# Last layer: one unread bf16 product ahead of each half score tile and of each bank of distance products

## The chip, the cores and the metric

The program runs on one core of one Trainium2 chip. The metric is the device time of one execution in microseconds; lower is better. A core has five engines with a queue each: TensorE (PE; its weight loads are shown as PEld), VectorE (DVE), ScalarE (ACT), GpSimd (POOL) and SyncE (SP), which here only issues DMAs. An engine works through its queue in order; engines wait for each other through semaphores. TensorE writes into PSUM, which has banks of 512 float32 per partition; VectorE and ScalarE read it.

## The reference: what is computed

Four layers run one after the other over an activation `x` of 4 sequences, 1024 tokens and 128 channels. Each layer is `x = x + s * silu(f)`, where `s` is an attention or a recurrence and `f` a feed-forward block over the normalised `x`. Only the last layer (layer 3) is changed. Its attention has 16 heads of 8 channels, is causal, and adds a term for the relative distance of two tokens:

```python
srel = srel_skew(jnp.einsum('bhnd,hmd->bhnm', qx, ex))      # products with distances, then a shift by rows
qk = (jnp.einsum('bhnd,bhmd->bhnm', qx, kx) + srel) * inv_dim
mask = 1000000000.0 * jnp.triu(jnp.ones((n, n), dtype=x.dtype), 1)
atten = jax.nn.softmax(qk - mask, axis=-1)
out = jnp.einsum('bhnm,bhmd->bhnd', atten, vx).transpose(0, 2, 1, 3).reshape(b, n, d)
return out @ Wp.T + bp
```

The table of distances has 256 entries, so each query tile of 128 tokens needs distance products of 256 columns, while its scores have up to 1024 columns.

## The kernel before

Layers 0 to 2 fill the first part of the span; the first instruction of layer 3's attention on TensorE starts 2151.5 us after the span's start. Layer 3 (`layer3`, L1736) works on 16 groups: 4 sequences (`b`) by 4 sets of heads (`i`), 4 heads at a time (`j`), whose 32 channels each (8 channels split into high and low parts, both in float32r) lie in a 32-row strip of the tiles `q` and `k`. Within a group, 8 query tiles `t` of 128 tokens are taken in the order 7, 0, 6, 1, 5, 2, 4, 3 (L1733); these are the 128 units (L1759).

**Scores.** `scores3` (L2077) goes through a unit's key columns in tiles of 512: two for `t` above 3, one otherwise, so 12 in a group and 192 in the layer. Each tile takes two PSUM buffers `sc` of two banks (L2095), one for heads 0 and 1, one for heads 2 and 3: a half score tile is one such buffer. All `sc` buffers there are is two (L2240), so the products of the next tile (L2097, one for each head, 32 rows by up to 512 columns) can only start when VectorE has read the same half of the tile before. VectorE reads each head's scores, adds the distance term `rel`, and finds the row's minimum of the negated scores (L2106, L2113). ScalarE then takes the exponential (L2120).

**Weights times values.** `transpose` (L1793) has VectorE turn the exponentials into tiles `wT` (L1807), and `weigh3` (L2126) multiplies them by the values with small float32 products into 32-column strips of `po` (L2134). The `wT` tiles have one buffer of each size, so a transpose may wait for earlier products. A float32 product is two instructions on TensorE.

**Distances.** `relative3` (L2021) is called 8 times for each group, seven parts ahead of the unit that needs it (L1862): two PSUM banks `pr` from the three `tr` buffers (L2029), in each two products of 32 rows by 256 columns (L2033), copied to `r` by ScalarE (L2035), stored to HBM (`flat`, L2038 and L2039) and read back in a sheared form as `rel` (`shear3`, L2042, L2054 to L2060), where GpSimd fills the masked parts (L2064).

**Beside these** run the feed-forward block (`ffn3`, L1972) in four pieces in the units of the second group of each sequence, the projections of the next sequence (`begin3`, L1933), and `finish3` and `end3` (L2142, L2158), which close a group and a sequence.

**What sets the order.** The loop of L1839 writes the products of a score tile, then a transpose and part of the weighing, then the comparison of that tile. The framework that builds the program keeps data dependencies and buffer reuse but may place independent instructions of one engine in another order, by its own estimate of when each can run. The trace shows that it does so: the first score product runs at 2155.08 us between distance products, although the source writes seven parts of distances ahead of it (L1785).

Of the kernel before, what the change touches and what calls it, by code (L numbers as in the profile page):

```python
# [11 lines left out]
BF16 = mybir.dt.bfloat16  # L12
# [8 lines left out]
P = 128  # L21
# [1714 lines left out]
def layer3(k, W, x3, out, eps5, ps, first):  # L1736
# [11 lines left out]
    nc, tc = k.nc, k.tc  # L1748
    with ExitStack() as st:
        pool = lambda name, bufs, **kw: st.enter_context(tc.tile_pool(name=name, bufs=bufs, **kw))  # L1750
        p1, p2, temp, dram = pool("l3", 1), pool("l3d", 2), pool("l3r", 3), pool("rel3", 6, space=DRAM)
        pairs = []
        for n in range(2):
            q, kk = p1.tile([P, 1 + T], F32R, tag=f"q{n}", name="q"), p1.tile([P, T], F32R, tag=f"k{n}", name="k")
            nc.vector.memset(q[:, 0:1].bitcast(F32), 0.0)
            pairs.append((q, kk))
        vb = p1.tile([P, 32, 4, 4, 8], F32, tag="vb", name="vb")
        nc.gpsimd.memset(vb, 0.0)
        units = [(b, i, t) for b in range(NB) for i in range(4) for t in ORDER3]  # L1759
        batch, group, flats, rels = {}, {}, {}, {}  # L1760

        def part(h):

            at, h = divmod(h, 8)
            if at < 4 * NB:
                pair = ORDER3[h // 4 * 4 + h // 2 % 2] // 2
                if h % 2 == 0:
                    flats[at, pair] = dram.tile([P, 4, 2, 384], F32, tag="flat", name="flat")
                relative3(k, W, temp, ps, flats[at, pair], group[at]["q"], at % 4, pair, h % 2)

        def ahead(n):
            if n < len(units):
# [2 lines left out]

        def stream():
            for n, (b, i, t) in enumerate(units):
                yield from scores3(k, p1, p2, ps, group[n // 8], rels.pop(n), t)

        batch[0] = {"qk": first["qk"], "vd": first["vd"], "xnT": p1.tile([P, T], F32, tag="xnT", name="xnT")}  # L1780
        nc.sync.dma_start(out=batch[0]["xnT"], in_=first["xnT"])
# [3 lines left out]
        for n in range(7):  # L1785
            part(n)
            if n in (1, 3):
                ahead(n // 2)
# [45 lines left out]

        tiles = [(n, first) for n, (b, i, t) in enumerate(units) for first in range(0, (t + 1) * P, 512)]
        fill = stream()
        next(fill)
        next(fill)
        for x, (n, first) in enumerate(tiles + [(len(units), 0)] * 4):  # L1839
# [8 lines left out]
            b, i, t = units[n]  # L1848
            at, pos = n // 8, n % 8
# [9 lines left out]
            if pos == 0:  # L1859

                next(project, None)
            part(n + 7)  # L1862
            if pos == 2:
                next(project, None)
# [153 lines left out]
        nc.gpsimd.tensor_copy(vb[rows, :, :, a, :], v[rows].rearrange("p n (j d) -> p n j d", d=8))  # L2018


def relative3(k, W, temp, ps, flat, q, i, pair, jp):  # L2021

    nc = k.nc
    r = temp.tile([P, 2, 2, 256], F32, tag="temp", name="r")
    js = (2 * jp, 2 * jp + 1)
    pr = [ps.tile([P, 2, 256], F32, tag="tr", name="pr") for _ in js]  # L2029
    for m in range(2):  # L2030
        for j, to in zip(js, pr):
            at, t = slice(32 * j, 32 * j + 32), 2 * pair + m
            nc.tensor.matmul(to[:, m, :], q[at, t * P : (t + 1) * P], W["emb"][at, i, :], start=True, stop=True)  # L2033
    for n, to in enumerate(pr):
        nc.scalar.copy(r[:, n], to)  # L2035
    rows = flat[:, 2 * jp : 2 * jp + 2].rearrange("p j m u -> p (j m) u")
    r = r.rearrange("p j m u -> p (j m) u")
    nc.sync.dma_start(out=rows[:, :, 0:256], in_=r)  # L2038
    nc.sync.dma_start(out=rows[:, :, 256:384], in_=r[:, :, 0:P])  # L2039
# [34 lines left out]
    return rel  # L2074


def scores3(k, p1, p2, ps, group, rel, t):  # L2077

    nc = k.nc
    q, kk = group["q"], group["k"]
    n = (t + 1) * P
    at = lambda j: slice(32 * j, 32 * j + 32)
    size = "b" if t > 3 else "s"
    S = [(p2 if t > 3 else p1).tile([P, T if t > 3 else 512], F32, tag=f"S{size}{j}", name="neg") for j in range(4)]
    group["S", t] = S
    low = [p2.tile([P, 3], F32, tag=f"low{j}", name="low") for j in range(4)]  # L2090
    least = [3e38] * 4
    plain = max(0, t - 4) * P
    for first in range(0, n, 512):
        last = min(first + 512, n)
        halves = [ps.tile([P, 2, 512], F32, tag="sc", name="score") for _ in range(2)]  # L2095
        for j in range(4):
            nc.tensor.matmul(  # L2097
                halves[j // 2][:, j % 2, 0 : last - first], q[at(j), 1 + t * P : 1 + n], kk[at(j), first:last], start=True, stop=True
            )
        yield "products"  # L2100
        for j in range(4):
            sc = halves[j // 2][:, j % 2]

            neg, m = S[j], low[j]
            if first < plain:
                nc.vector.tensor_scalar(  # L2106
                    neg[:, 0:plain], sc[:, 0:plain], -INV3, None, op0=ALU.mult, op1=ALU.min, accum_out=m[:, 0:1]
                )
                least[j] = m[:, 0:1]
            begin = max(first, plain)  # L2110
            slot = min(t, 4) - t + begin // P
            here = m[:, 1:2] if first == 0 else m[:, 2:3]
            nc.vector.tensor_tensor_reduce(  # L2113
                out=neg[:, begin:last], in0=sc[:, begin - first : last - first],
                in1=rel[:, j, slot : slot + (last - begin) // P, :].rearrange("p s c -> p (s c)"),
                scale=-INV3, scalar=least[j], op0=ALU.add, op1=ALU.min, accum_out=here,
            )
            least[j] = here
            if last == n:
                nc.scalar.activation(  # L2120
                    neg[:, 0:n], neg[:, 0:n], AF.Exp, bias=here, scale=-1.0, accum_out=group["sums"][:, j, t : t + 1]
                )
        yield "compared"
# [70 lines left out]
def tile_kernel(ctx: ExitStack, tc: tile.TileContext, I, out):  # L2194
# [44 lines left out]
    with last, ExitStack() as st:  # L2239
        ps = PsumTags(st, tc, {"sc": 2, "tr": 3, "o": 1}, "ps3")  # L2240
        layer3(k, W3, x3, out, eps5, ps, first)
# [20 lines left out]
```

## Time and profile before

| What | Value |
|---|---|
| Runs shown (3) | 3174.36, 3178.16 and 3178.8 us; median 3178.16 us |
| The profiled execution's own time | 3175.99 us |
| Its span, first to last instruction | 3174.2 us, so 1.8 us lie around it |
| Granted TensorE clock over the span | 0.738 of full |
| Layer 3's stretch from 2150 to 3130 us | 980 us; busy: PE 717.84, PEld 479.63, DVE 770.02, ACT 669.23, POOL 307.24 |
| Granted clock in that stretch | 0.68 |
| DMA in that stretch | busy share 0.77, 235 GB/s |
| Score products in that stretch (L2097) | 756 instructions, 217.5 us busy, mean 588 ns |
| Distance products (L2033) | 512 instructions, 125.8 us busy, mean 426 ns |
| Weighing products (L2134) | 9683 instructions, 254.0 us busy, mean 253 ns |

How to read the profile: an engine's busy time is the time in which at least one of its instructions is recorded as running. The records of products overlap, since each contains a fixed latency and products follow each other into the array. The granted clock is the share of full speed that the chip's throttle allowed TensorE. The view of lines gives for each group of instructions its count, its busy time and mean duration, and then the idle time of the engine just before, with what ended it. The view of waits turns this around: who waited for whom, how long in all, how many times, and the longest.

### The profile page before, as it was taken

The numbers are of one execution on the slowest core, as the hardware profiler recorded it, in microseconds if no ns is written. First come the engines' busy times: TensorE is split into PE (matmuls) and PEld (weight loads), VectorE is DVE, ScalarE is ACT, GpSimd is POOL, SyncE is SP. The second block draws the span as 40 slices with busy tenths as digits, with TensorE's granted clock in tenths as the row PEclk, the third lists the DMA queues.
The fourth block names the chain that finished last, engine by engine and source line by source line (L and its number), as shares of the span: only waits on it lengthen the run. The fifth ranks groups of instructions, "written<-read, shape, count | busy, mean of one in ns | idle before, by whom it ended". The sixth has DMA issues, their size and how long they took to land. (4 is left out here: it accounts for less than half of the span.)

```text
span 3174.2 us, 47753 instructions
## 1 busy us (share of the span) xinstructions
PE 2163.6 (68%) x17039; PEld 1256.8 (40%) x17041; DVE 2291.8 (72%) x5558; ACT 1542.6 (49%) x3300; POOL 1167.5 (37%) x1094
## 2 busy tenths in 40 slices
PE   5777777577887776794543574375777777777865
PEld 2555555232332232562210122253544544544543
DVE  5554544878888786656778888676788797687777
ACT  3554544333333333535432463145765775775773
POOL 3433444144444434123477433232333332323322
PEclk9888888588888887895655566565766666766666
DMA  3000000100000000230334356339588588678772
GB/s 78 16 1 1 1 1 1 35 0 0 0 0 0 7 7 7 103 110 20 74 92 114 123 120 136 100 118 295 174 256 272 176 268 261 197 242 269 215 242 66
DMA packets 334065, 333.13 MB, mean 105 GB/s; under 512 B 25968, under 2 KB 307436, under 8 KB 328196
## 3 DMA queue, kind: packets, MB, share of 16 engines
q1 hardware_dynamic: 332676, 325.90, 34.6%
q10 hardware_dynamic: 1152, 4.19, 0.4%
q8 instruction: 134, 2.20, 0.3%
q14 instruction: 103, 0.84, 0.1%
HBM read 175.31 MB, written 154.14 MB: 104 GB/s over the span
## 5 line engine op out<-in xcount | busy, mean ns | idle before, releaser
L2120 ACT ACTIVATE neg<-neg,low 128x640 f32<-128x640 f32 (+7 forms) x512 | 390.7, 766 | 105.8 <-DVE low L2113 104.6
L1807 DVE STREAM_TRANSPOSE wT<-neg 128x640 f32<-128x640 f32 (+7 forms) x512 | 366.3, 754 | 50.3 <-PE po L2134 45.5
L2064 POOL TENSOR_SCALAR_AFFINE_SELECT rel<-rel 128x512 f32<-128x512 f32 x288 | 180.5, 638 | 551.4 <-DMA rel<-flat 412.6
L2134 PE MATMUL po<-wT,vb 128*32 128x64 f32 (+1 forms) x10240 | 266.2, 253 | 71.9 <-issue 40.8
L2097 PE MATMUL score<-k,q 32*128 32x512 f32 (+3 forms) x768 | 220.5, 587 | 124.6 <-DVE low L2113 121.3
L2134 PEld LDWEIGHTS po<-wT,vb 128*32 128x32 f32 x10240 | 210.9, 134 | 144.5 <-issue 84.1
L2113 DVE CUSTOM_DVE_ANT_0 neg<-score,rel,low 128x128 f32<-128x128 f32 (+3 forms) x448 | 213.0, 510 | 71.4 <-PE score L2097 29.3
L2035 ACT COPY r<-pr 128x512 f32<-128x512 f32 x256 | 135.2, 584 | 126.4 <-PE pr L2033 79.8
L2113 DVE CUSTOM_DVE_ANT_0 neg<-score,rel 128x512 f32<-128x512 f32 (+3 forms) x320 | 150.6, 520 | 50.4 <-POOL rel L2064 21.2
L2097 PEld LDWEIGHTS score<-k,q 32*128 32x128 f32 x768 | 96.8, 247 | 214.1 <-DVE low L2113 139.6
L837 PE MATMUL pg<-xnT,w 128*128 128x512 f32 x256 | 149.1, 666 | 7.1 <-DVE h L841 4.0
L2033 PE MATMUL pr<-emb,q 32*128 32x256 f32 x512 | 125.8, 426 | 39.7 <-ACT r L2035 25.5
L840 ACT ACTIVATE h<-pg 128x512 f32<-128x512 f32 x128 | 75.9, 596 | 157.5 <-PE pg L837 154.1
L790 POOL TENSOR_TENSOR prod<-rest,kv 128x2048 f32<-128x2048 f32 x32 | 145.5, 4598 | 18.4 <-ACT rest L780 18.4
L839 PE MATMUL pu<-xin,w 128*128 128x512 f32 x256 | 140.5, 632 | 12.9 <-DVE h L841 7.4
L828 PE MATMUL po<-h,w 128*128 128x512 f32 x256 | 129.8, 628 | 26.5 <-DVE h L841 26.5
L216 PE MATMUL pt<-ident,three 128*24 128x128 bf16 x64 | 9.2, 295 | 196.6 <-DVE three L213 196.6
L2033 PEld LDWEIGHTS pr<-emb,q 32*128 32x128 f32 x512 | 89.0, 262 | 74.4 <-ACT r L2035 38.9
L433 PE MATMUL px<-hT,xbcT 128*128 128x512 f32 x256 | 115.0, 593 | 0.0
L1086 PE MATMUL ph<-xin,upT 128*128 128x512 bf16 (+1 forms) x126 | 68.3, 572 | 66.4 <-DVE xin L1080 64.0
L1491 PE MATMUL read<-kt,const_sb 128*128 128x128 f32 x256 | 51.1, 372 | 90.3 <-POOL kt L1486 90.3
L785 DVE TENSOR_REDUCE s<-prod 128x128 f32<-128x2048 f32 x32 | 73.1, 2284 | 49.6 <-POOL prod L790 49.6
(633 smaller groups left out, 5775.7 us busy)
## 6 DMA issues: line engine op xcount, KB each, us to landing
flat<-r SPq DMA_DIRECT2D x128, 512.0 KB
rel<-flat SPq DMA_DIRECT2D x112, 512.0 KB
flat<-r SPq DMA_DIRECT2D x128, 256.0 KB
rel<-flat SPq DMA_DIRECT2D x96, 256.0 KB
kt<-kd SPq DMA_DIRECT2D x16, 512.0 KB
qt<-qd SPq DMA_DIRECT2D x16, 512.0 KB
kdc<-kdd SPq DMA_DIRECT2D x16, 512.0 KB
ktc<-ktd SPq DMA_DIRECT2D x16, 512.0 KB
```

Source lines behind the costliest of these rows:

```text
L790: nc.gpsimd.tensor_tensor(prod, attn.rearrange("p (t h g) -> p t h g", t=4, g=16)[:, t].unsqueeze(2).to_broadcast(each), kv[:, t, 1, :].re ...
L828: nc.tensor.matmul(po, W["w2"][:, e, c, :], h[:, c, :], start=(e == 0 and c == 0), stop=(e == 7 and c == 1))
L837: nc.tensor.matmul(pg, W["w1"][:, e, c * P : (c + 1) * P], xnT, start=True, stop=True)
L839: nc.tensor.matmul(pu, W["w3"][:, e, c * P : (c + 1) * P], xin, start=True, stop=True)
L1807: nc.vector.transpose(weights[at, pair][j][:, t % 2, 0 : (t + 1) * P], S[j][:, 0 : (t + 1) * P])
L2033: nc.tensor.matmul(to[:, m, :], q[at, t * P : (t + 1) * P], W["emb"][at, i, :], start=True, stop=True)
L2035: nc.scalar.copy(r[:, n], to)
L2064: nc.gpsimd.affine_select(out=rel[:, :, slot(back), :], in_=rel[:, :, slot(0), :], compare_op=op, fill=fill, base=0, pattern=[[0, 4], [-si ...
L2097: nc.tensor.matmul(halves[j // 2][:, j % 2, 0 : last - first], q[at(j), 1 + t * P : 1 + n], kk[at(j), first:last], start=True, stop=True)
L2113: nc.vector.tensor_tensor_reduce(out=neg[:, begin:last], in0=sc[:, begin - first : last - first], in1=rel[:, j, slot : slot + (last - begi ...
L2120: nc.scalar.activation(neg[:, 0:n], neg[:, 0:n], AF.Exp, bias=here, scale=-1.0, accum_out=group["sums"][:, j, t : t + 1])
L2134: nc.tensor.matmul(o[32 * j : 32 * j + 32, 2 * pair + m.start : 2 * pair + 2, :], vb[:, kb % 4 * NT + kb // 4, j].rearrange("p a d -> p (a ...
```

## The change

A tile `ones` of 512 bf16 columns is filled once by GpSimd at the layer's start, just behind the fill of `vb` (L1758). A function `beat` multiplies the bf16 identity `ident16`, which is there already (L103), by `ones` into a whole PSUM bank. Nobody reads what it writes: the product that follows starts its own sum in the same bank. One beat is written ahead of each half score tile (for heads 0 and 2, into the half's first bank), two at the start of each call of `relative3`, one for each of its two banks. That is 2 x 192 = 384 and 2 x 128 = 256, together 640 beats, each with a weight load of its own.

```diff
         vb = p1.tile([P, 32, 4, 4, 8], F32, tag="vb", name="vb")
         nc.gpsimd.memset(vb, 0.0)
+        ones = p1.tile([P, 512], BF16, tag="ones16", name="ones")
+        nc.gpsimd.memset(ones, 1.0)
+
+        def beat(bank):
+
+            nc.tensor.matmul(bank, k.ident16, ones, start=True, stop=True)
+
...
     pr = [ps.tile([P, 2, 256], F32, tag="tr", name="pr") for _ in js]
+    for to in pr:
+        beat(to.rearrange("p m u -> p (m u)"))
     for m in range(2):
...
         halves = [ps.tile([P, 2, 512], F32, tag="sc", name="score") for _ in range(2)]
         for j in range(4):
+            if j % 2 == 0:
+                beat(halves[j // 2][:, 0])
             nc.tensor.matmul(
```

The other lines of the diff only hand `beat` on to `relative3` and `scores3`.

More of the change, by code (lines that the diff above doesn't have):

```diff
@@ L1768, in part @@
                     flats[at, pair] = dram.tile([P, 4, 2, 384], F32, tag="flat", name="flat")
-                relative3(k, W, temp, ps, flats[at, pair], group[at]["q"], at % 4, pair, h % 2)
+                relative3(k, W, beat, temp, ps, flats[at, pair], group[at]["q"], at % 4, pair, h % 2)
         def ahead(n):
@@ L1777, in stream @@
             for n, (b, i, t) in enumerate(units):
-                yield from scores3(k, p1, p2, ps, group[n // 8], rels.pop(n), t)
+                yield from scores3(k, beat, p1, p2, ps, group[n // 8], rels.pop(n), t)
         batch[0] = {"qk": first["qk"], "vd": first["vd"], "xnT": p1.tile([P, T], F32, tag="xnT", name="xnT")}
@@ L2018, in values3, with relative3 @@
         nc.gpsimd.tensor_copy(vb[rows, :, :, a, :], v[rows].rearrange("p n (j d) -> p n j d", d=8))
-def relative3(k, W, temp, ps, flat, q, i, pair, jp):
+def relative3(k, W, beat, temp, ps, flat, q, i, pair, jp):
     nc = k.nc
@@ L2074, in shear3, with scores3 @@
     return rel
-def scores3(k, p1, p2, ps, group, rel, t):
+def scores3(k, beat, p1, p2, ps, group, rel, t):
     nc = k.nc
```

## The prediction, made before the changed kernel ran

> **What bounds the kernel now.** First the page's busy shares and its slices, then the stretch of layer 3 (2150 to 3130 us) by lines, by waits of VectorE, and by windows.
>
> ```profile
> PE 2163.6 (68%) x17039; PEld 1256.8 (40%) x17041; DVE 2291.8 (72%) x5558; ACT 1542.6 (49%) x3300; POOL 1167.5 (37%) x1094
> ...
> DVE  5554544878888786656778888676788797687777
> ...
> PEclk9888888588888887895655566565766666766666
> ```
>
> The change touches only layer 3, the last 13 of the 40 slices. There VectorE is 70 to 90% busy and TensorE's granted clock is 0.6 to 0.7. In the 980 us VectorE works 770.02 us, more than any other engine. So the end is set by VectorE's work plus its idle time, and the change can act only through that idle time. Its causes:
>
> ```profile
> DVE wT L1807 <- PE po L2134: 45.5, 15, 8.7
> DVE neg L2113 <- POOL rel L2064: 43.5, 13, 12.0
> DVE neg L2113 <- PE score L2097: 31.2, 23, 4.1
> DVE neg L2113 <- issue: 26.9, 12, 3.1
> DVE neg L2106 <- PE score L2097: 20.1, 16, 9.3
> DVE on L2155 <- PE pr L2153: 12.6, 11, 2.7
> ```
>
> Columns: total us, times, longest. TensorE ends 45.5 us of the waits by its weighing products, 51.3 us by score products, 12.6 us by finishing a group. In the 43.5 us, the distance terms come late from HBM; there TensorE is not the cause.
>
> **What the clock follows.** The granted clock is 0.50 or 1.00 and changes only every 3.41 us. Windows cut at those places (columns: PE, PEld, DVE, ACT, POOL busy with counts, clock, DMA share, GB/s):
>
> ```profile
> 2305.40:2308.81 3.41, 3.41 (x86) 2.47 (x76) 1.52 (x7) 0.37 (x1) 1.57 (x2) 0.50 0.65 236
> 2308.81:2312.23 3.42, 3.06 (x18) 1.87 (x16) 3.42 (x10) 3.06 (x6) 3.20 (x4) 1.00 0.38 134
> 2312.23:2315.64 3.41, 1.27 (x5) 0.57 (x4) 3.41 (x14) 2.46 (x5) 1.86 (x3) 0.50 1.11 364
> ...
> 2325.88:2329.29 3.41, 3.41 (x96) 2.74 (x88) 3.41 (x17) 3.39 (x7) 0.56 (x1) 0.50 0.37 108
> 2329.29:2332.71 3.42, 3.42 (x152) 2.56 (x155) 2.89 (x13) 3.38 (x7) 0.00 (x0) 1.00 1.11 228
> ```
>
> The first window is full and the clock rises after it. The second has PE busy 3.06 of 3.42 us, yet the clock falls after it. What differs is how much of the array was used. The second holds 12 distance and 4 score products, each of 32 rows only. Count work in beats: 512 columns once through the whole array are 1; a float32 instruction counts its columns twice (L1983's pairs of 256 columns follow each other every 0.43 us at full clock); 32 rows or 32 columns count a quarter. A score product of 512 columns is then 0.25, a distance product 0.125, a weighing product of 64 columns 0.0625. The first window holds about 6.0, the second 2.3, that of 2325.88 about 5.8. Over all windows of layer 3, a line at 5.0 to 5.2 beats in a window separates "full next" from "half next" with 4 exceptions in 299. That is the working rule here: about 5.1 beats of array work in 3.41 us.
>
> [...]
>
> **Work before and after.** By shapes and counts of the stretch: weighing 545, feed-forward 192 and 96, scores 142, L2166 96, distances 64, the rest 114, together 1249 beats in 287 windows, or 4.35 a window, below the line. The change adds 640 beats, to 6.6 on average. The work is uneven, so I went through the windows, adding one beat at every second score product and two at every fourth distance product. The share of windows above the line goes from 39% to 66%. So the clock should go from 0.68 to about 0.83, not to 1.
>
> **The price of a beat.** The nearest row is layer 2's bf16 product of 512 columns:
>
> ```profile
> L1086 PE MATMUL ph<-xin,upT x126: 376/609/634, 1471.0 to 1917.3; 128*48 128x512 bf16 x64, 128*128 128x512 bf16 x62
> ```
>
> Minimum, median and maximum in ns. The minimum is at full clock, the median at half, so halving adds 609 - 376 = 233 ns: one pass takes about 0.23 us at full clock and 0.47 at half, the rest is latency that overlaps. 640 beats are 149 us at full clock, 301 at half. The weight loads (95 to 151 ns in the same view) lie beside running products, except where the queue stood empty, which the bounds below include. A beat also parts the four score products: four score products of 512 columns now run beside each other (0.50 us for four at 2515.64, full clock); with a beat between the halves only two can.
>
> **Part by part.**
>
> 1. *Beats ahead of scores (384).* TensorE waits there for VectorE to free the half, then does beat and products while VectorE goes on with the other half and with transposes (355.3 us over 192 tiles, 1.85 us a tile). That hides most of them. Going through the 192 tiles, the time between the end of a half's products and VectorE's first use is under 0.25 us in 39 tiles for the first half and in 28 for the second, under 0.45 in 45 and 41. Lengthening each by its beat alone at full clock exposes 9 us; by 0.47 us, and twice that for the second half, 50 us. Where the clock rises, the products themselves shorten (512 columns: mean 783 ns at half clock, 504 at full), which pays for a beat. With the clock that the window count gives, 15 us are exposed. I take **+15**, bounds 9 to 50.
>
> 2. *Beats ahead of distances (256).* They are needed seven parts later, but everything behind them on TensorE's queue waits: score products, weighing, the feed-forward block. 60 of them fall into idle times of VectorE that TensorE or the feed-forward block ends; 60 x 0.23 to 0.47 = 14 to 28 us if each is on the path, 0 if TensorE would have waited for ScalarE's copy anyway (L2033's groups stood 64.4 us for `r`). I take **+15**, nearer the first because these queues are mostly full (in the 8.7 us wait before 2526.3, six us are TensorE's).
>
> 3. *The clock.* TensorE's work at half clock inside VectorE's idle times that TensorE ends is 70 us (40 ahead of scores, 24 ahead of L1807, 6 ahead of L2155). About half of the cold windows turn (39 to 66% above the line), and a product then takes 0.64 (scores) to 0.71 (weighing, 222 for 312 ns) of its time: 70 x 0.5 x 0.35 = **-12**. Bounds: 0, and -37 if all turn and the other idle times (33 us cold) shrink as well. Outside these idle times faster products gain nothing, VectorE's own work hides them.
>
> 4. *The rest, 0.* The fill of `ones` stands on POOL behind that of `vb` (3.51 us for 4096 columns, done at 2150.4); 512 columns are under 0.5 us and the first product waits for `q` until 2151.5. 1280 more instructions on TensorE's stream are 4%. The order of instructions is laid out anew with 640 more products; I know no sign for that and add 10 us to either side.
>
> Sum: 15 + 15 - 12 = +18 on 3176.0 us of the profiled execution (span 3174.2 and 1.8 around it), **3194**. The median of the runs is 2.2 us above that execution, inside their spread.
>
> **Rivals.**
>
> *The clock wins (faster).* Place: the queue of TensorE in layer 3. If reordering and feedback bring nearly every window with work above 5.1 beats, every beat costs 0.23, step 1 is 9, step 2 half hidden at 7, step 3 is -37: 3176 + 9 + 7 - 37 = 3155. It decides from a granted clock of about 0.9 in the stretch. For it: the line is clear, and the window of 2308.81, with its three calls of distance products, rises from 2.3 to about 10 beats. Against it: beats wait in the same queue as the products, so a window in which TensorE waits (as 2312.23, 1.27 us busy) stays cold.
>
> *Beats at half clock (slower still).* If the array's constant operands do not count, or the windows stay below the line, the clock stays near 0.7: step 1 is 50, step 2 is 28, step 3 is 0: 3254. For it: TensorE's 717.84 us would go to nearly all of the 980, and `wT`'s single buffers pass that on.
>
> *Nothing.* The unread product is dropped, or the three steps cancel: about 3177.
>
> **How the numbers follow.** My forecast 0.43, the clock wins 0.28, half clock 0.18, nothing 0.11. The bounds of the forecast's own terms reach from -28 to +78; leaving out the outer ends, the range is 3150 to 3238. The measurement tells about 0.2% (6.4 us) from no change. Faster by more: 0.27, nearly all of the first rival. Within: the third rival and a corner of the forecast, 0.15. Slower by more: 0.58.
>
> **What would show it.** The stretch's clock at 0.80 to 0.86; TensorE's busy time there above 718, near 780; weighing products (254.0 us now) below 225; the waits for score products above 51 us; waits of L1807 for `po` little changed. Wrong would be a clock of 0.9 or more with VectorE's idle time below 190 us, or a clock still at 0.70.

## The result and the profile after

The changed kernel takes 3233.77 us (median of 4 runs, 3229.74 to 3236.3), the kernel before 3178.36 us (3174.36 to 3178.8): ratio 1.0176, 95% interval 1.0158 to 1.0194. It is about 55 us slower, where 18 were forecast. The profiled execution took 3236.3 us, span 3234.2.

Three lines of the page of after that answer to those of before:

```profile
PE 2366.5 (73%) x17681; PEld 1279.5 (40%) x17681; DVE 2297.2 (71%) x5558; ACT 1545.1 (48%) x3300; POOL 1166.6 (36%) x1095
...
DVE  5555545878878886657868878557777777777777
...
PEclk9888888688778878985655665567778877877876
```

VectorE's work is as before (2297.2 us against 2291.8), so nearly all of the 55 us is idle time of VectorE (from 2150 us to the end, summed over the trace: 225 us before, 282 after). TensorE is 203 us busier. The clock in layer 3 went up by about one tenth. The view of windows of after, in the stretch for which the prediction gave a clock (columns as there):

```profile
2150.00:3130.00 980.00, 870.04 (x11323) 477.83 (x11322) 722.35 (x2334) 641.44 (x1425) 291.70 (x388) 0.77 0.73 224
```

The clock is 0.77 instead of 0.68, not 0.80 to 0.86. TensorE is busy 870 us there, not 780. VectorE gets through less work in the same time, 722 instead of 770 us. What VectorE waits for in after (us in all, times, longest; 2150 to 3190 us, which holds about the work that before did from 2150 to 3130):

```profile
DVE neg L2124 <- PE score L2108: 58.2, 52, 3.2
DVE neg L2124 <- issue: 56.2, 27, 6.7
DVE neg L2117 <- PE score L2108: 43.5, 26, 15.1
DVE wT L1814 <- PE po L2145: 29.2, 19, 4.7
DVE neg L2124 <- POOL rel L2073: 25.4, 8, 8.8
```

Added lines shift the numbers: L2117, L2124, L2108, L1814 and L2145 are L2106, L2113, L2097, L1807 and L2134 of before. Waits for score products doubled (51.3 to 101.7 us) and so did those without a visible releaser (26.9 to 56.2). Waits of the transposes for weighing products (`po`) fell from 45.5 to 29.2. The beats and the weighing, by the view of lines of after in the same stretch (busy us, mean ns of one):

```profile
L2145 PE MATMUL po<-wT,vb 128*32 128x64 f32 (+1 forms) x9680 | 229.1, 246 | 45.8 <-issue 28.3 <-DVE wT L1814 14.0 <-DVE ln_mv L139 3.0
...
L1764 PE MATMUL score<-ones,ident 128*128 128x512 bf16 x378 | 181.4, 480 | 49.1 <-DVE low L2124 47.6
L1764 PE MATMUL pr<-ones,ident 128*128 128x512 bf16 x254 | 115.4, 484 | 7.8 <-ACT r L2044 4.3 <-ACT v L1972 2.0 <-DVE on L2166 0.8
```

Weighing went from 254.0 to 229.1 us: the faster clock is real. At first sight this explains why the waits for `po` fell. The experiments show that it does not.

**What one beat holds.** Four timelines of TensorE (two here, those of e3 and e15 further down) show the same work, calls of distance products at half clock: four products, two in each of two banks. First before, then after (start, length, and in brackets the idle time ahead with what ended it):

```profile
2163.58 1.28 PE L2033 MATMUL pr<-emb,q 32*128 32x256 f32 x4 [5.33 <-ACT r L2035]
2165.68 1.28 PE L2033 MATMUL pr<-emb,q 32*128 32x256 f32 x4 [0.82 <-ACT r L2035]
```

```profile
2162.57 0.58 PE L1764 MATMUL pr<-ones,ident 128*128 128x512 bf16 x1 [1.36 <-ACT r L2044]
2163.09 0.79 PE L2042 MATMUL pr<-emb,q 32*128 32x256 f32 x2
2163.81 0.61 PE L1764 MATMUL pr<-ones,ident 128*128 128x512 bf16 x1
2164.35 0.79 PE L2042 MATMUL pr<-emb,q 32*128 32x256 f32 x2
2165.07 0.61 PE L1764 MATMUL pr<-ones,ident 128*128 128x512 bf16 x1
```

Before, a call takes 1.28 us and the next starts after 2.10, since ScalarE's copies set the pace; TensorE has 0.82 us to spare. After, a call takes 2.50 us (2162.57 to 2165.07) without a gap: nothing is left to spare on TensorE's queue. The four products, one span before, are now two pairs. ScalarE is not held up in this place: in both kernels its copies come every 2.1 us, and wait for the store of an older `r` (one pair of copies before, one after):

```profile
2165.04 1.07 ACT L2035 COPY r<-pr 128x512 f32<-128x512 f32 x2 [1.02 <-DMA flat<-r]
```

```profile
2164.05 1.07 ACT L2044 COPY r<-pr 128x512 f32<-128x512 f32 x2 [1.04 <-DMA flat<-r]
```

Over the whole stretch, however, ScalarE waits longer for distance products, first before, then after (97.6 us in e12 below, which has the order of after without beats):

```profile
ACT r L2035 <- PE pr L2033: 79.8, 26, 21.0
```

```profile
ACT r L2044 <- PE pr L2042: 146.6, 58, 21.5
```

Over the whole trace of after, the time from a beat's start to the next beat's start, where two beats follow each other, is about 0.22 us at full clock and 0.40 at half (medians of 30 pairs each), which is the streaming that was priced at 0.23 and 0.47. But to the next 32-row product it is 0.32 and 0.536 (medians of 322 and 246). The difference is 0.10 to 0.14 us. The weight loads of those products wait with them, longer than before (for no visible releaser; before it was 58.1 us for score products and 21.6 for distance products):

```profile
PEld score L2108 <- issue: 143.9, 370, 1.8
PEld pr L2042 <- issue: 87.8, 199, 1.8
```

The loads of 32-row products behind a beat start 0.318 us after the beat's start at full clock and 0.535 at half, together with the product (medians of 312 and 234, where one clock holds for both). Between two beats lies a weight load too, of the whole array: it starts 0.01 us after the first beat's start, and the 0.22 us to the next beat show no cost of it; nor does the load of the 12 whole-array float32 products that follow a beat at full clock (0.22 us as well). So the price stands only where a 32-row product follows a beat on all rows. Theory 1 of e1 below puts it down to the rows that the beat holds; whether the load makes it or the switch between the two shapes, no run tells apart.

### The profile page after: what moved, and what is told of

Its sections match the earlier page's. It is cut to its first block, busy times and chain, and to the rows that moved or that the text cites. A ratio compares the mean times of both kernels' runs of the same rounds, so it can differ in the third digit from the quotient of the medians.

```text
span 3234.2 us, 48936 instructions
## 1 busy us (share of the span) xinstructions
PE 2366.5 (73%) x17681; PEld 1279.5 (40%) x17681; DVE 2297.2 (71%) x5558; ACT 1545.1 (48%) x3300; POOL 1166.6 (36%) x1095
## 5 line engine op out<-in xcount | busy, mean ns | idle before, releaser
L1814 DVE STREAM_TRANSPOSE wT<-neg 128x640 f32<-128x640 f32 (+7 forms) x512 | 365.4, 755 | 31.6 <-PE po L2145 29.2
L2145 PE MATMUL po<-wT,vb 128*32 128x64 f32 (+1 forms) x10240 | 240.5, 246 | 50.2 <-issue 28.8
L2124 DVE CUSTOM_DVE_ANT_0 neg<-score,rel,low 128x128 f32<-128x128 f32 (+3 forms) x448 | 213.9, 511 | 87.2 <-PE score L2108 36.3
L2145 PEld LDWEIGHTS po<-wT,vb 128*32 128x32 f32 x10240 | 196.7, 130 | 102.8 <-issue 66.1
L1764 PE MATMUL score<-ones,ident 128*128 128x512 bf16 x384 | 184.4, 480 | 52.0 <-DVE low L2124 50.4
L2124 DVE CUSTOM_DVE_ANT_0 neg<-score,rel 128x512 f32<-128x512 f32 (+3 forms) x320 | 152.9, 523 | 87.1 <-issue 37.8
L2108 PE MATMUL score<-k,q 32*128 32x512 f32 (+3 forms) x768 | 210.0, 538 | 0.0
L2108 PEld LDWEIGHTS score<-k,q 32*128 32x128 f32 x768 | 87.9, 223 | 147.7 <-issue 146.3
L2042 PE MATMUL pr<-emb,q 32*128 32x256 f32 x512 | 136.1, 410 | 0.1
L1764 PE MATMUL pr<-ones,ident 128*128 128x512 bf16 x256 | 116.4, 485 | 16.9 <-POOL ones L1760 9.1
L1764 PEld LDWEIGHTS <-ident 128*128 128x128 bf16 x640 | 60.6, 101 | 159.8 <-issue 73.3
```

The lines of the kernel that those rows point to most:

```text
L1764: nc.tensor.matmul(bank, k.ident16, ones, start=True, stop=True)
L1814: nc.vector.transpose(weights[at, pair][j][:, t % 2, 0 : (t + 1) * P], S[j][:, 0 : (t + 1) * P])
L2108: nc.tensor.matmul(halves[j // 2][:, j % 2, 0 : last - first], q[at(j), 1 + t * P : 1 + n], kk[at(j), first:last], start=True, stop=True)
L2124: nc.vector.tensor_tensor_reduce(out=neg[:, begin:last], in0=sc[:, begin - first : last - first], in1=rel[:, j, slot : slot + (last - begi ...
L2145: nc.tensor.matmul(o[32 * j : 32 * j + 32, 2 * pair + m.start : 2 * pair + 2, :], vb[:, kb % 4 * NT + kb // 4, j].rearrange("p a d -> p (a ...
```

## The experiments

Every kernel computes the same outputs. Their inserted lines shift the line numbers by a few. "Ratio" is to the kernel before on the same chip. The order in which each engine gets its instructions depends on how long the framework thinks they take, so a kernel with other beats is also laid out in another order. I therefore made most changes after the order was fixed. "New order" is that of the changed kernel. "Short order" is the one laid out for beats of 8 columns; it differs from the order before the change in 288 of TensorE's 10179 places and 20 of VectorE's 5371, while the new order differs in 1945 and 254.

| Kernel | Order | Beats | Median us | Ratio (95%) |
|---|---|---|---|---|
| after | new | 640, 512 columns, whole array | 3233.77 | 1.0176 (1.0158 to 1.0194) |
| e1 | its own | ahead of scores only | 3185.70 | 1.0034 (1.0021 to 1.0047) |
| e2 | its own | ahead of distances only | 3190.11 | 1.0039 (1.0021 to 1.0057) |
| e3 | new | cut to 8 columns | 3176.74 | 1.0008 (0.9993 to 1.0023) |
| e4 | short | widened to 512 | 3302.83 | 1.0402 (1.0374 to 1.0431) |
| e5 | short | 8 columns | 3225.55 | 1.0157 (1.0135 to 1.0179) |
| e6 | short | widened ahead of scores only | 3258.71 | 1.0269 (1.0245 to 1.0294) |
| e7 | short | widened ahead of distances only | 3272.25 | 1.0300 (1.0281 to 1.0320) |
| e8 | its own | scores only, not tied to the half tile | 3180.96 | 1.0018 (1.0007 to 1.0028) |
| e9 | short | 8 columns on 32 rows, two loads | 3241.78 | 1.0203 (1.0182 to 1.0223) |
| e10 | new | 8 columns on 32 rows, two loads | 3215.13 | 1.0115 (1.0086 to 1.0145) |
| e11 | new | 512 columns on 32 rows, two loads | 3269.62 | 1.0291 (1.0257 to 1.0324) |
| e12 | new | none | 3152.84 | 0.9929 (0.9909 to 0.9949) |
| e13 | short | none | 3175.72 | 1.0001 (0.9986 to 1.0016) |
| e14 | new | 8 columns on 32 rows, one load | 3182.97 | 1.0014 (1.0002 to 1.0026) |
| e15 | new | 512 columns on 32 rows, one load | 3185.61 | 1.0029 (1.0017 to 1.0041) |
| e16 | new | ahead of scores only | 3193.96 | 1.0051 (1.0034 to 1.0068) |
| e17 | new | ahead of distances only | 3195.86 | 1.0052 (1.0032 to 1.0071) |

**Each group alone, and the length: e1 to e4.** e1 and e2 leave out one of the two loops that call `beat`. e3 and e4 replace the beats' shapes once the order stands:

```diff
+                block.instructions[n] = copy.replace(i, ins=[of(i.ins[0]), i.ins[1]], outs=[of(i.outs[0])])   # of: other columns
```

> Only the 384 beats ahead of half score tiles; the 256 ahead of distance products are gone. Theory 1, price on the score path: a beat holds all rows of the array, so the weights of the next 32-row product cannot load beside it (in the changed kernel's trace the product starts 0.32 us after the beat at full clock and 0.54 at half, not 0.21 to 0.23 and 0.43 to 0.47), and VectorE waits for it wherever the cover is short: most of the 55 us stays, 3210 to 3225 us. Theory 2, load on TensorE's queue as a whole: the loss goes by the number of beats, 0.6 of 55 us, about 3211, with the clock of the layer down to about 0.72. Theory 3, the new order of instructions: no forecast of size, since the order is laid out anew once more.

> Only the 256 beats ahead of the banks of distance products. Theory 1, score path: distances are needed seven parts later, so little is lost, 3180 to 3195 us. Theory 2, load on the queue: 0.4 of 55 us, about 3200. If the two halves of the change add up, this run's loss and that of the run with score beats alone make 55 us; if the clock's gain needs both, they make more.

> The order of instructions on every engine is that of the changed kernel, but after it is laid out all 640 beats are cut from 512 to 8 columns. Order theory: the loss stays, 3225 us or more, since the clock's gain goes too. Streaming theory (the 512 columns cost): about 3180 to 3190. Turn theory (loading and unloading the whole array between 32-row products costs even without columns): a third to a half of the loss stays, 3195 to 3210. The layer's clock should fall back to about 0.68 in all of them.

> The reverse: the order is laid out with beats of 8 columns, which leaves VectorE's and ScalarE's order nearly that of the kernel before (20 of 5371 and 0 of 2737 places differ), and all beats are widened to 512 columns afterwards. Order theory: most of the loss goes, 3180 to 3195 us. Price theory (streaming and turns of the array): the loss stays, 3225 to 3240 us, with the layer's clock near 0.76 as in the changed kernel.

e1 costs 11 us, less than both of its theories, and e2 12, within that of the score path; together they make less than half of 55, but each has an order of its own, so the two do not add up to anything. e3 says that in the new order 512 columns instead of 8 make the whole loss (1.68%, 53 us by the difference of the ratios). e4, above both of its theories, says that in nearly the old order the same beats cost 128 us. So a new order that is worse is not the cause: for these beats the new order is better. The timeline of TensorE in e3, same place as above:

```profile
2163.26 0.17 PE L1766 MATMUL pr<-ones,ident 128*128 128x8 bf16 x1 [4.29 <-ACT r L2046]
2163.36 0.79 PE L2044 MATMUL pr<-emb,q 32*128 32x256 f32 x2
2164.08 0.19 PE L1766 MATMUL pr<-ones,ident 128*128 128x8 bf16 x1
2164.20 0.79 PE L2044 MATMUL pr<-emb,q 32*128 32x256 f32 x2
2165.38 0.17 PE L1766 MATMUL pr<-ones,ident 128*128 128x8 bf16 x1 [0.39 <-ACT r L2046]
```

The short beats part the four products into two pairs just as the long ones do, but a call takes 1.73 us (2163.26 to 2164.20 + 0.79) and the next starts after 2.12, as before.

**Presence and length in the short order, and the tie to the half tile: e5 to e8.** e8 sends each score beat as two of 256 columns into the unread half of `po`'s bank, so that it doesn't wait for VectorE to free the half score tile:

```diff
+            for _ in range(2):
+                tc.keep_in_program_order(nc.tensor.matmul(spare, k.ident16, ones[:, 0:256], start=False, stop=True, skip_group_check=True))
```

> All 640 beats are laid out and run with 8 columns, in nearly the order of the kernel before. The trace of the run that was cut after layout shows 0.10 to 0.12 us from a beat of 8 columns to the next product, 70 us on TensorE's queue in all. Streaming theory (the time goes to the 512 columns): within 0.3% of before, 3170 to 3185 us. Turn theory: 3190 or more. Either way it is the base for the run that was widened after layout (3303 us), whose order it has.

> Same order; after layout only the 384 beats ahead of half score tiles are widened to 512 columns, those ahead of distance products stay at 8. If the loss of 125 us in this order goes by count, 75 us: about 3250. Score-path theory (VectorE waits for a tile whose beats come after the wait for PSUM): 3260 to 3280. Queue theory (what counts is what the distance calls push back): below 3220.

> Same order; only the 256 beats of the distance calls are widened. By count 50 us: about 3225. Score-path theory: 3180 to 3200. Queue theory: 3240 or more. If this loss and that of the run with widened score beats make less than 125 us together, the beats share the cover that hides one of them but not both.

> Beats with the work of those ahead of scores alone, but written into the unread half of the bank of the weighing products (two of 256 columns each), so that a beat need not wait for VectorE to free the half score tile and can run while TensorE waits. Theory that the place behind the wait costs: 3155 to 3178 us, below the run with score beats alone (3186) and perhaps below the kernel before, since the clock's gain stays. Theory that any 512 columns on the queue cost: 3186 or more, as with score beats alone.

Beats of 8 columns cost 1.6% here, widening those ahead of scores 1.1%, those ahead of distances 1.4%, all of them 2.5%: the groups add up. (e5 is where the turn theory puts it, e6 between the count and the score path, e7 where the queue theory puts it.) e8 lies a little below e1 (1.0018 against 1.0034, the intervals just overlap) and between its two theories. Each of the two has an order of its own, and orders differ by more than that here, so what waiting together with the half tile costs is not shown. Why short beats cost 50 us here and nothing in e3 was open.

**On 32 rows, with a fault: e9 to e11.** Each beat keeps its place, but runs on the strip of the product behind it:

```diff
+                    ins=[rows(i.ins[0], j, columns), rows(i.ins[1], j, P)],
+                    tile_size=(32, P),
+                    tile_position=(32 * j, 0),
+                    ldweights=True,
```

> The order laid out for 8-column beats; there 8-column beats of the whole array gave 3225.55 us, ratio 1.0157. Here each beat has the same place and the same 8 columns, but uses only the 32 rows of the strip on which the product behind it runs, so that three of the four strips are free beside it. Theory 'turn': a beat of the whole array parts products that otherwise overlap on their own strips, whatever its length, and this costs the 50 us: expect 3172 to 3190 us. Rival 'order': the 50 us come from the new places of VectorE's and TensorE's instructions: expect 3215 to 3235 us. In between, each has its share.

> The order of the changed kernel, with beats of 8 columns on 32 rows. Cut to 8 columns of the whole array the same order gave 3176.74 us, ratio 1.0008. Theory 'turn': what the turns cost there (up to 50 us, by the other order) was paid for by a better order, so without them this one beats both kernels: expect 3125 to 3165 us. Rival 'order': 8-column beats cost nothing in either form, and the order of the changed kernel is worth the same as the one before: 3170 to 3183 us.

> The changed kernel with each beat on 32 rows and all its 512 columns: a quarter of the array's work, and the other three strips free. Theory 'turn and length on the whole array': most of the 55 us go, since products on other strips run beside the beat; 3160 to 3200 us, and a clock in layer 3 hardly above the 0.68 of before. Rival 'the length on TensorE's queue alone': each beat still holds its own strip and its bank for 0.23 us at full and 0.47 us at half clock, and the product behind it waits as long as before: 3215 to 3245 us.

All three came out above both theories. They have a fault: the framework had given each beat a separate weight load for the whole array, and it stayed in, beside the strip's own. So these three don't test what their expectations say. They became useful beside e14 and e15, where that load is gone.

**The order alone, and one load: e12 to e15.** e12 and e13 take the beats and their loads out of the finished order and put a beat's waits on the product behind it:

```diff
+                i = copy.replace(i, sync_info=mybir.SyncInfo(on_wait=list(waits.values()), on_update=list(info.on_update)))
```

> The order of the changed kernel on every engine, with the 640 beats and their weight loads taken out after the order was laid out; their waits are on the product behind them. Theory 'price and order': the order is better than the old one by about what a short beat costs, so without beats it runs at 3115 to 3145 us. Rival 'length only': short beats cost nothing and the order is worth nothing, 3168 to 3184 us.

> The order laid out for beats of 8 columns (288 of TensorE's and 20 of VectorE's places differ from the order before the change), the beats taken out. Theory 'price and order': this is the old order in all that matters, 3172 to 3184 us, and the beats of 8 columns cost the 50 us. Rival 'places': the few places cost the 50 us, 3210 to 3230 us.

> The order of the changed kernel, beats of 8 columns on the 32 rows of the product behind them, with one load of weights for a beat (the earlier strip runs had two). Beats of 8 columns of the whole array gave 3176.7 us here, the strip with two loads 3215.1. Theory 'turn of the whole array': 3125 to 3160 us. Rival 'a beat costs its weight load and its place in the queue, on any rows': 3170 to 3190 us.

> The same with 512 columns; the whole array gave 3233.8 us, the strip with two loads 3269.6. Theory 'turn of the whole array': products on other strips run beside the beat, 3170 to 3205 us. Rival 'place in the queue': 3225 to 3250 us, since its own product waits as long; the granted clock in layer 3 stays at 0.65 to 0.70, as a beat here is a quarter of the array's work.

e13 is the kernel before to 0.2%, so its few other places cost nothing and the short beats of e5 cost the 50 us. e12 lies between its two expectations: the new order is worth 0.71% (23 us, by the interval 16 to 29), and e12 is faster than both kernels. Some of VectorE's waits in e12 (2150 to 3113 us):

```profile
DVE neg L2126 <- PE score L2110: 39.3, 24, 5.5
...
DVE neg L2119 <- PE score L2110: 19.9, 8, 9.9
DVE wT L1816 <- PE po L2147: 19.1, 18, 2.9
```

The last line (L1807 of before) matters most: with the new order and no beat the waits for `po` are 19.1 us, against 45.5 in the old order. The same line in e13, the old order without beats, and in e3, the new order with short ones (2150 us to the end):

```profile
DVE wT L1816 <- PE po L2147: 43.9, 11, 8.8
```

```profile
DVE wT L1816 <- PE po L2147: 27.8, 21, 2.7
```

In the six kernels of the short order this wait is 43.9 to 51.2 us, with and without beats, in the nine of the new order 16.5 to 31.2. So the fall to 29.2 in after is the order's doing; within the one order, the beats raised this wait by 10 us (one trace each), in spite of the faster clock.

e14 equals e3 within 0.1% (1.0014 and 1.0008), so for short beats it does not matter whether they use 32 rows or all: the "turn of the whole array" falls for them, and e14 is where its rival puts it. For long ones the rows decide. e15's beats have all 512 columns, and yet cost only 0.15% more than e14's short ones; those of the whole array cost 1.68% more than e3's. The timeline of TensorE in e15, same place as above:

```profile
2164.08 0.60 PE L1766 MATMUL pr<-ones,ident 32*128 32x512 bf16 x1 [6.62 <-ACT r L2047]
2164.13 0.77 PE L2045 MATMUL pr<-emb,q 32*128 32x256 f32 x1
2164.57 0.60 PE L1766 MATMUL pr<-ones,ident 32*128 32x512 bf16 x1
2164.62 0.98 PE L2045 MATMUL pr<-emb,q 32*128 32x256 f32 x3
2166.20 0.60 PE L1766 MATMUL pr<-ones,ident 32*128 32x512 bf16 x1 [0.60 <-ACT r L2047]
```

A call with both beats takes 1.52 us (2164.08 to 2164.62 + 0.98) and leaves 0.60 idle, so the next starts after 2.12 us, at ScalarE's pace as before. Beats and products lie over each other. e15's beats stand in the same places and write as many columns of the same banks as those of after; what they lack is three quarters of the rows. The price of the length is therefore that the product behind a beat on all rows starts late: in these timelines 0.52 and 0.54 us after the beat's start in after, 0.05 in e15. The granted clock, in windows of e3, e14 and e15, in this order:

```profile
2150.00:3130.00 980.00, 827.38 (x12140) 559.59 (x12139) 771.76 (x2505) 671.94 (x1502) 306.75 (x412) 0.65 0.76 235
```

```profile
2150.00:3130.00 980.00, 728.78 (x12048) 498.23 (x12048) 760.54 (x2473) 664.42 (x1488) 305.55 (x407) 0.65 0.76 234
```

```profile
2150.00:3130.00 980.00, 762.41 (x12039) 489.71 (x12039) 759.82 (x2459) 663.04 (x1482) 305.18 (x407) 0.68 0.76 233
```

512 columns instead of 8 raise it by 0.03 on 32 rows (0.65 to 0.68, as much as e12 has without beats) and by 0.12 on all rows (0.65 to 0.77): a quarter of the rows, a quarter of the gain.

The separate loads can now be priced: e10 against e14, a load of the whole array between 32-row products, 640 times, 1.0% or 32 us; e11 against e15, the same where the strip's beat has 512 columns, 2.6% or 83 us.

**The two groups in one order: e16 and e17.** As e12, but one group of beats stays.

> The order of the changed kernel; the 384 beats ahead of scores as they are, the 256 ahead of distances taken out after the order was laid out. Without any beat this order takes 3152.8 us, with all 3233.8. Theory 'the groups add up, in the shares that widening them showed (33 to 46 us)': 3182 to 3192 us. Rival 'step 1 was right at 15 us and step 2 alone was wrong': 3163 to 3173 us. Rival 'they make each other worse': this and the next kernel together lie 20 us or more below the sum of 81.

> The same order; the 256 beats ahead of distances as they are, the 384 ahead of scores taken out. Theory 'the groups add up': 3195 to 3206 us. Rival 'step 2 was right at 15 us': 3163 to 3173 us. Rival 'they make each other worse': 3165 to 3185 us here, and the two kernels' losses against 3152.8 add up to 61 us or less.

Against e12, the beats ahead of scores cost 1.22% and those ahead of distances 1.23%, 39 us each, known to about 8 us; together 78, and after minus e12 is 2.47%, 78. They add up, to within about 12 us, so the rival that they make each other worse falls for this order (e16 lies 2 us above the range of adding up, e17 inside). The smaller losses of e1 and e2 come with orders of their own.

## Why the prediction was wrong

By differences of ratios, times 3178 us, the change is: order -23, beats ahead of scores +39, beats ahead of distances +39, sum +55. The direction was right, by the forecast's own mechanism (beats lie ahead of work that VectorE waits for), and the time lies near the upper end of the stated range. The sizes were not right: the step that failed is the price of the beats in steps 1 and 2, the part of it that was taken as hidden. 15 + 15 us were expected, 78 measured. That the miss is not larger is luck: the new order, which the sum put at nothing, took 23 us back.

**Steps 1 and 2.** Beats ahead of scores cost 39 us instead of 15, inside the bounds of 9 to 50. Beats ahead of distances cost 39 instead of 15, above the bound of 28. Both measured figures are net of whatever the clock gave back. Of the 78 us, 53 come with the 512 columns on the whole array (after against e3); on 32 rows, where other strips run beside the beat, the same columns cost 5 (e15 against e14). So TensorE's queue does not hide a beat that takes all rows as well as the two steps assumed. The other 25 us are there with 8 columns too.

Two sentences of the price are wrong or unused, and they explain part of this at most. "The weight loads (...) lie beside running products": in the stretch of before that holds for 478 of their 479.6 us, but the load of a 32-row product behind a beat starts only with its product (after), 0.32 and 0.536 us after the beat instead of the 0.23 and 0.47 of the price. For the 322 such beats at full clock and the 246 at half that is 235 us on TensorE's queue instead of 190. "With a beat between the halves only two can": it was written down and never put into the sum. By itself it does not show in the time: the short beats of e3 part the products too, and those of e14, on strips, do not, and the two kernels differ by 0.1%. With long beats, what is due to their columns and what to the parted strips is not told apart; at half clock e3's call (parted, short) takes 1.73 us, e15's (long, not parted) 1.52, and only that of after, which is both, 2.50, more than the 2.1 between ScalarE's copies.

**Step 2 besides** looked only at the idle times that VectorE had already, 60 of 256 beats. The traces show what that leaves out: new ones. At half clock a call of distance products leaves TensorE no time to spare, and what stands behind the calls is late. VectorE's first comparison of layer 3 starts at 2160.00 us in after, at 2155.78 in e12, the same order without beats. The time to spare was also overrated: the 64.4 us for which the distance products stood for `r` add up waits of the weight loads (38.9 us) and of the products behind them (25.5 us, 28 times), which can be the same time seen on two queues.

**Step 3, the clock, -12: not seen.** The rule behind it held in the main: 512 columns of the whole array raise the clock from 0.65 (e3) to 0.77, 512 on 32 rows from 0.65 (e14) to 0.68, so the clock follows the array work, and an unread product with a constant operand counts. The line at 5.1 beats is less sharp than it looked: with each product weighed as in the prediction and counted in the window in which it starts, 10 of 299 windows break it before and 24 of 316 after. The gain should have shown where VectorE waits for weighing, 24 of the step's 70 us, and ahead of scores, 40 of them, where the beats' own cost lies over it. The first wait is 29.2 us with 512 columns and 27.8 with 8 (e3); on strips, where the clock gains only 0.03, it is 22.2 (e15) and 27.7 (e14), one trace each. No kernel here raises the clock without adding work, so what 0.09 of clock is worth by itself stays open.

**Step 4, the rest, 0 with 10 to either side: -23 for the order.** "I know no sign for that" still holds; the bound was too small. By the ratios one order costs 128 us with the 640 beats and the other 56, a difference of 72, of which 23 are the order's own and 49 that it fits these beats better. The framework spaces work by what it thinks each product takes, so products that cost time also change where all others stand. The sum of steps 1 to 3 was made in the order of before, where the measured sum is +128 (e4).

One reading ahead of the sum was loose, without effect on it: of the last 13 slices two have VectorE at 60 to 70%, and the first has a clock of 0.5.

Of the rivals, "beats at half clock" (3254) came nearer in size for a reason that did not hold: the constant operands do count, and most beats (364 of 640) ran at full clock. "The clock wins" fails with its own condition, a clock of 0.9.

**Still open:** what 8 columns cost 25 us for (new order) or 50 (short order). A load alone costs 32 (e10 against e14), so a load by itself would be enough to explain it, but no run has a beat without one. Why the new order is better without beats is not tested either; that it shortens the waits for `po` (45.5 to 19.1 us) is all that the trace shows.

## What to carry to other kernels

A product of 512 bf16 columns on the whole array kept the next product on a 32-row strip from starting for 0.32 us at full clock and 0.536 at half (after), 0.10 and 0.14 more than such a product keeps the next one of its own kind: price it from its start to the start of the next strip product, and ask whether the queue that it stands in still has that much to spare. Where a program is laid out by estimated durations, a change that adds instructions has two effects, and they are told apart by editing the instructions after the order is fixed; the order found here by accident is a faster kernel without the beats (3152.84 us). A higher granted clock is no gain by itself: here 0.09 more of it came with work that cost 78 us net in the same order, in a kernel whose end is set by another engine.

## What the runs showed of the hardware

- 512 bf16 columns on one 32-row strip, 640 times, cost 0.15% more than 8 columns (e15, e14), and in the timeline of e15 the product behind starts 0.05 us after the beat; on the whole array 1.68% more (after, e3).
- From a whole-array bf16 product of 512 columns to a 32-row product behind it are 0.32 us at full clock and 0.536 at half; to another whole-array product, with a weight load between, about 0.22 and 0.40 (after).
- 640 weight loads of the whole array, without any product that uses them, cost 32 us among 32-row products, and 83 us where 512-column beats on 32 rows are among these (e10 and e11 against e14 and e15).
- An unread product of ones counts for the clock, by the share of the array that it uses: 512 columns instead of 8 raise it from 0.65 to 0.77 on all rows (e3, after) and from 0.65 to 0.68 on 32 rows (e14, e15).
